# Attention times a gated network on one core: two projections moved behind the last layer, the warming matmuls split, weight blocks moved on GpSimd

## The chip, the cores and the metric

The kernel runs on one NeuronCore of one Trainium2 chip. A NeuronCore has a matrix engine (TensorE, PE in the profile; PEld is its weight load), a vector engine (VectorE, DVE), a scalar engine (ScalarE, ACT), a fourth compute engine (GpSimd, POOL) and a queue that here issues the transfers (SyncE, SP). Each takes its own instructions in order, and they wait for one another by semaphores. SBUF is the working memory, PSUM the memory that TensorE writes.

The metric is device time in microseconds (us), the median over runs. The profile is of one execution, and its span is shorter than that execution's device time by what lies around it.

## The reference

For each of 8 sequences of 512 tokens with 256 features:

```
xn = layernorm(x)
q, k, v = split(xn @ in_proj_w.T)          # 16 heads of 16; q and k are rotated by position
s  = softmax(mask(q k^T / 4)) v            # key at or before the query, fewer than 250 back
s  = s @ out_proj_w.T
h  = relu(s0 * [xn, -xn] @ K0) * 2         # K0, K1, K2 hold +1 or -1
h  = relu(s1 * h @ K1) * 2
g  = silu(s2 * h @ K2)
out = x + s * g
```

Everything is float32.

## The kernel before

**Tiles.** A sequence is worked on transposed: features on the 128 partitions, its 512 tokens along the row. The token tiles of 128 that come in and go out are numbered t = 0 to 3. The layers of the gated network take each weight block twice, against the high half of the activations (float16, names ending in h) and against the low rest (names ending in l), and both products are summed in PSUM. So there are two copies of each sign matrix: w1h and w1l, w2h and w2l.

**Order.** The function run() orders the program. Every piece of work is a triple: planned time in us, its cost on TensorE, and a function that issues instructions. The pieces are sorted by planned time; a piece may return follow-ups with a delay, which wait in a heap until the plan's clock has passed them. The order that comes out is the order on each engine's queue; the planned times are the author's numbers and are not measured. A sequence takes SEQ = 42 plan units; L1, L2 and L3 are the plan's costs of a block of the first, second and third layer.

**PSUM.** The pool ps_m has three buffers (tag "mm"), which almost all products outside attention share: xnT (the transposes), ka, kb, qa, qb (the projections of k and q, two halves each), v_ps, h_ps, z_ps and att_ps. A product can begin only when the buffer that it is given has been emptied. ps_o has one buffer for the attention values.

**The start.** make_identity builds ident on GpSimd. warm (L206) runs 16 matmuls of ident by itself. VectorE takes the mean and variance (stats) and normalises each token tile (norm, L250, name xn), TensorE transposes it (turn_x, xnT_ps), and ScalarE and VectorE take the copies xT, xh and xl out of PSUM. VectorE builds w0h from bytes (make_w0). project() computes ka, kb, qa, qb; VectorE multiplies each by the two rows of the rotation table (L319, names m_ka, m_kb, m_qa, m_qb), and GpSimd's rotate (L339) combines m_ka with m_kb, and m_qa with m_qb. m_kb and m_qb share one buffer, so m_qb can be written only when the rotation of k has read m_kb. ScalarE rounds the rotated k and q (kh, qh, L356), VectorE takes the rests (L363), and they go through DRAM to be laid out for the heads.

make_w1 (L174) turns the bytes of the second layer's weights, kb1, into blocks of w1h or w1l of 128x1024: on ScalarE or on GpSimd (L180). make_w2 (L182) does the same for the third layer on GpSimd (w2h, w2l). Their places are the list at L846. GpSimd also masks the attention's probabilities (L640, L647).

**The end.** For all sequences but the last, the third layer z_ps of a sequence runs inside the next sequence. In the last one (b = 7) the second layer is done in two halves of 256 tokens, each followed by the third layer of its two token tiles. last() (L429) computes z_ps. For t = 0 and 1, VectorE scales it into gate, and gate_ready() forms the sigmoid: exponential on ScalarE, plus one on GpSimd, reciprocal on VectorE (L505), product on GpSimd (L506). project_o() (L778) computes att_ps, the output projection, and loads x again as xr; the product with gate is taken on VectorE (L795), the sum with xr on GpSimd (L800), and SyncE stores the tile (L801). For t = 2 and 3 ("final") the projection is done before z_ps and copied out as att (L791), and behind z_ps follow on VectorE: the product of z_ps, scale and att (L451), the reciprocal (L461), a product (L462) and a sum (L463), and the store (L464). late() (L518) gives the projections' planned times: for the last sequence

```
        if b + 1 == B:
            return SEQ * b + 40.0 + 0.9 * t
```

xr has two buffers: the load for tile 2 waits until tile 0 has been summed.

Of the kernel before, what the change touches and what calls it, by code (L numbers as in the profile page):

```python
# [11 lines left out]
F32 = mybir.dt.float32  # L12
# [4 lines left out]
ALU = mybir.AluOpType  # L17
# [17 lines left out]
def tile_attention_times_gated_ffn(  # L35
# [37 lines left out]
    nc = tc.nc  # L73
    P = 128
    B, T, E = x.shape
    H = HEADS
    D = E // H
    NT = T // P
# [14 lines left out]
    work = ctx.enter_context(tc.tile_pool(name="work", bufs=2))  # L93
# [109 lines left out]

    quick = set()

    def warm():  # L206

        pw = ps_m.tile([P, P], F32, tag="mm", name="warm")
        for n in range(16):
            nc.tensor.matmul(pw, ident, ident, start=(n == 0), stop=(n == 15))  # L210

    def run(pieces):
        clock, count_, due = 0.0, itertools.count(), []
# [215 lines left out]
    def last(b, t, how):  # L429
        st = states[b]  # L430
        pz = ps_m.tile([P, E], F32, tag="mm", name=f"z_ps_{b}_{t}")
        if how == "at once":
            for c in range(NF1):
                nc.tensor.matmul(
                    pz, st["h2p"][:, c, ts(t, P)], w2["l"][:, c].bitcast(F32),
                    start=(c == 0), stop=(c == NF1 - 1),
                )
        else:
            for p in "hl":
                for c in range(NF1):  # L440
                    nc.tensor.matmul(  # L441
                        pz, st["h2" + p][:, c, ts(t, P)], w2[p][:, c],
                        start=(c == 0 and p == "h"), stop=(c == NF1 - 1 and p == "l"),
                    )
        gate = st["gate", t] = outs.tile([P, E], F32, tag=f"gate{t}", name=f"gate_{b}_{t}")
        if how == "final":
            den = denominator(b, t)

            def ends():
                nc.scalar.activation(den, pz, AF.Exp, scale=scales[:, 1:2])  # L450
                nc.vector.scalar_tensor_tensor(  # L451
                    gate, pz, scales[:, 0:1], st["att", t], ALU.mult, ALU.mult
                )
                return [(0.5, add)]

            def add():
                nc.scalar.activation(den, den, AF.Identity, bias=1.0)
                return [(0.4, final)]

            def final():  # L460
                nc.vector.reciprocal(den, den)  # L461
                nc.vector.tensor_tensor(gate, gate, den, ALU.mult)  # L462
                nc.vector.tensor_tensor(gate, gate, st["xr", t], ALU.add)  # L463
                nc.sync.dma_start(out[b, ts(t, P), :], gate)  # L464

            return [(0.0, ends)]

        def scale():
            nc.vector.tensor_scalar(gate, pz, scales[:, 0:1], None, ALU.mult)
            if how != "later":  # L470
                return [(0.5, lambda: gate_ready(b, t))]

        return [(0.0, scale)]

# [45 lines left out]

    def late(b, t):

        if b + 1 == B:
            return SEQ * b + 40.0 + 0.9 * t
        return SEQ * (b + 1) + (32.0 + 3.2 * t if b + 2 < B else 18.0 + 2.5 * t)
# [252 lines left out]
    def project_o(b, t, final=False):  # L778
        st = states[b]
        pp = ps_m.tile([P, E], F32, tag="mm", name=f"att_ps_{b}_{t}")  # L780
        for c in range(EC):
            nc.tensor.matmul(  # L782
                pp, st["V", c][:, ts(t, P)], wo_sb[:, c, :],
                start=(c == 0), stop=(c == EC - 1),
            )
        xr = work.tile([P, E], F32, tag="xr", name=f"xr_{b}_{t}")
        nc.sync.dma_start(xr, x[b, ts(t, P), :])
        st["xr", t] = xr
        if final:
            att = st["att", t] = work.tile([P, E], F32, tag="xn", name=f"att_{b}_{t}")  # L790
            return [(0.0, lambda: nc.scalar.copy(att, pp))]  # L791

        def product():
            y = st["gate", t]
            nc.vector.tensor_tensor(y, pp, y, ALU.mult)  # L795
            return [(0.5, store)]

        def store():
            y = st.pop(("gate", t))
            nc.gpsimd.tensor_tensor(y, y, xr, ALU.add)  # L800
            nc.sync.dma_start(out[b, ts(t, P), :], y)  # L801

        return [(0.0, product)]
# [31 lines left out]
    def swap():  # L835
# [2 lines left out]
        outs = ctx.enter_context(tc.tile_pool(name="outs", bufs=1))  # L838

    everything = [  # L840
        (-38.5, 0, signs), (-40.5, 0, warm),
        (18.2, 0, make_w2), (22.5, 0, swap), (SEQ * (B - 1) + 45.0, 0, add_up),
    ]
    for c in range(EC):
        everything.append((-30 + 0.1 * c, 0, lambda c=c: make_w0(c)))
    for w, f, at, engine in (  # L846
        ("l", 0, -20, nc.gpsimd), ("l", 1, -19, nc.gpsimd), ("l", 2, -18, nc.gpsimd),
        ("h", 0, -17, nc.scalar), ("h", 1, -16, nc.scalar), ("h", 2, 5, nc.gpsimd),
        ("l", 3, 9.0, nc.gpsimd), ("l", 4, 9.1, nc.gpsimd), ("l", 5, 9.2, nc.gpsimd),
        ("l", 6, 9.3, nc.gpsimd), ("l", 7, 9.4, nc.gpsimd), ("h", 3, 15.2, nc.scalar),  # L850
        ("h", 4, 17.0, nc.scalar), ("h", 5, 18.7, nc.scalar), ("h", 6, 20.4, nc.scalar),
        ("h", 7, 22.2, nc.scalar),
    ):
        everything.append((at, 0, lambda f=f, w=w, e=engine: make_w1(f, w, e)))
# [139 lines left out]
```

## Time and profile before

| | |
|---|---|
| Device time, three runs | 629.59, 631.65, 631.93 us; median 631.65 |
| Profiled execution, device time | 632.4 us |
| Its span | 630.6 us |
| TensorE busy | 609.6 us, 97% of the span |
| VectorE busy | 393.0 us, 62% |
| GpSimd busy | 316.1 us, 50% |
| ScalarE busy | 300.0 us, 48% |
| Largest group, L415 h_ps by float32 halves of w1 | 576 matmuls of 392 ns mean |
| GpSimd waits for ScalarE's p before a mask (L640), longest | 9.1 us |

The busy time of an engine is how long some instruction of it ran, and the share is that of the whole span. A mean share doesn't say which engine a given stage waits for; that is read from the waits (who waited, for whom, how long), from the timeline (start in us from the span's start, length, engine, source line, operation, output<-inputs, and in brackets the idle time before it and what ended it), and from the chain (the work that ended last, followed back). The table by stretch gives, for stretches of time, each engine's busy us and number of instructions, the clock granted to TensorE as a share of full speed, and the share and speed of the transfers. A float32 matmul appears as two passes.

### The profile page before, as it was taken

The page shows a single profiled execution, that of the slowest core. Times are in us where ns is not written, and L with a number is a line of the kernel's source. Part 1 is how long each engine was busy: PE and PEld are TensorE (multiplying, and loading weights), DVE is VectorE, ACT ScalarE, POOL GpSimd, SP SyncE. Part 2 cuts the span into 40 slices and gives each one's busy share as a digit, 9 for nine tenths or more (in the row PEclk, how much of TensorE's full clock was granted, in tenths as well). Part 3 has the DMA queues.
Part 4 walks back from the last instruction along what each step waited for, and adds up shares of the span by engine and source line. Part 5 has one row for each costly group of instructions (what it writes and reads, how often), then busy time and mean ns, then how long its engine had stood idle before and what let it go on. Part 6 is the DMA issues. An engine that isn't in the chain of part 4 may idle for free.

```text
span 630.6 us, 12029 instructions
## 1 busy us (share of the span) xinstructions
PE 609.6 (97%) x4834; PEld 398.8 (63%) x4834; DVE 393.0 (62%) x668; ACT 300.0 (48%) x442; POOL 316.1 (50%) x406
## 2 busy tenths in 40 slices
PE   7899999999999999999999999999999999999993
PEld 5454566656665567755676566765676556777883
DVE  6582545757656674766758576485675668457664
ACT  3566564525455445535355454453444544564421
POOL 1945452356623566327644367234662356638630
PEclk9899999999999999999999999999999999999998
DMA  8261821125321163113521153402532116230101
GB/s 269 81 234 51 300 86 50 36 83 210 101 76 50 68 223 112 51 51 144 166 93 51 55 221 96 132 25 94 207 107 73 51 68 226 76 109 18 53 26 40
DMA packets 38193, 67.20 MB, mean 107 GB/s; under 512 B 5104, under 2 KB 19184, under 8 KB 38128
## 3 DMA queue, kind: packets, MB, share of 16 engines
q1 hardware_dynamic: 36384, 64.24, 30.2%
q10 hardware_dynamic: 1744, 2.10, 1.0%
q8 instruction: 40, 0.66, 0.4%
q14 instruction: 25, 0.20, 0.1%
HBM read 36.96 MB, written 29.36 MB: 105 GB/s over the span
## 4 chain that ended last, share of the span: by engine, by line
PE 84%; DVE 6%; DMA 4%; POOL 3%; ACT 2%; issue 1%; SPq 0%; POOLq 0%; ACTq 0%
PE h_ps L415 40%; PE po L679 11%; PE z_ps L441 9%; PE sc L605 7%; PE v_ps L292 4%; PE att_ps L782 4%; PE qa_ps L307 2%; PE kb_ps L307 2%; PE qb_ps L307 2%; DMA kb<-in_k_dram 2%; DMA xr<-in_x_dram 2%; PE ka_ps L307 2%; PE xnT_ps L268 1%; DVE den L505 1%; ACT p L624 1%
## 5 line engine op out<-in xcount | busy, mean ns | idle before, releaser
L624 ACT ACTIVATE p<-sc 128x1024 f32<-128x1024 f32 (+2 forms) x144 | 138.5, 1013 | 75.0 <-PE sc L605 41.0
L640 POOL TENSOR_SCALAR_AFFINE_SELECT p<-p 128x512 f32<-128x512 f32 x128 | 93.8, 739 | 106.5 <-ACT p L624 106.5
L415 PE MATMUL h_ps<-h1l,w1l_sb 128*128 128x512 f32 (+1 forms) x576 | 144.2, 392 | 0.0
L415 PE MATMUL h_ps<-h1h,w1h_sb 128*128 128x512 f16 (+1 forms) x576 | 123.0, 356 | 0.9 <-ACT v_pad L299 0.5
L415 PEld LDWEIGHTS h_ps<-h1l,w1l_sb 128*128 128x128 f32 x576 | 99.5, 188 | 25.7 <-issue 6.8
L426 ACT ACTIVATE h2h<-h_ps 128x512 f16<-128x512 f32 (+1 forms) x72 | 39.6, 550 | 136.5 <-PE h_ps L415 136.4
L415 PEld LDWEIGHTS <-w1h_sb 128*128 128x128 f16 x576 | 51.6, 98 | 55.8 <-issue 14.0
L647 POOL TENSOR_SCALAR_AFFINE_SELECT p<-p 128x512 f32<-128x512 f32 (+1 forms) x96 | 50.4, 525 | 58.0 <-ACT p L624 56.7
L679 PE MATMUL po<-p,v_pad 128*32 128x378 f32 (+4 forms) x1216 | 77.0, 372 | 1.6 <-DVE S L703 1.1
L424 DVE SCALAR_TENSOR_TENSOR h2l<-h_ps,h2h 128x512 fp32r<-128x512 f32 (+1 forms) x72 | 44.4, 617 | 52.0 <-ACT h2h L426 52.0
L505 DVE RECIPROCAL den<-den 128x256 f32<-128x256 f32 x30 | 52.5, 1749 | 26.0 <-POOL den L501 26.0
L424 DVE SCALAR_TENSOR_TENSOR h1l<-h_ps,h1h 128x512 fp32r<-128x512 f32 x64 | 42.5, 675 | 36.1 <-ACT h1h L426 36.1
L605 PEld LDWEIGHTS sc<-q,k 32*128 32x128 f32 x1216 | 44.1, 184 | 26.1 <-issue 15.0
L754 DVE RECIPROCAL S<-S 128x128 f32<-128x128 f32 x64 | 58.9, 934 | 0.0
L426 ACT ACTIVATE h1h<-h_ps 128x512 f16<-128x512 f32 x64 | 38.2, 597 | 43.0 <-PE h_ps L415 42.8
L605 PE MATMUL sc<-q,k 32*128 32x378 f32 (+4 forms) x1216 | 57.3, 306 | 0.0
L415 PE MATMUL h_ps<-xl,w0l_sb 128*128 128x512 f32 x128 | 53.6, 500 | 0.0
L679 PEld LDWEIGHTS po<-p,v_pad 128*32 128x32 f32 x1216 | 31.5, 109 | 30.8 <-issue 16.6
L800 POOL TENSOR_TENSOR gate<-gate,xr 128x256 f32<-128x256 f32 x30 | 23.1, 770 | 46.7 <-DMA xr<-in_x_dram 32.6
L415 PE MATMUL h_ps<-xh,w0h_sb 128*128 128x512 f16 x128 | 39.5, 391 | 0.1
L441 PE MATMUL z_ps<-w2l_sb,h2l 128*128 128x256 f32 x256 | 38.1, 291 | 0.0
L339 POOL TENSOR_TENSOR m_ka<-m_ka,m_kb 128x512 f32<-128x512 f32 x16 | 20.1, 1276 | 30.3 <-DVE m_kb L319 30.3
(95 smaller groups left out, 806.6 us busy)
## 6 DMA issues: line engine op xcount, KB each, us to landing
q<-dq SPq DMA_DIRECT2D x64, 256.0 KB, 3.5
dq<-qh SPq DMA_DIRECT2D x16, 512.0 KB, 3.4
dq<-m_qa SPq DMA_DIRECT2D x16, 512.0 KB, 4.6
k<-dk SPq DMA_DIRECT2D x32, 256.0 KB, 2.8
dk<-kh SPq DMA_DIRECT2D x8, 512.0 KB, 2.7
dk<-m_ka SPq DMA_DIRECT2D x8, 512.0 KB, 2.7
xr<-in_x_dram SPq DMA_DIRECT2D x32, 128.0 KB, 2.3
out_dram<-gate SPq DMA_DIRECT2D x32, 128.0 KB, 1.7
```

Source lines behind the costliest of these rows:

```text
L307: nc.tensor.matmul(ps, wqkv_sb[:, c, ds(col, P)], st["xT"][:, c, :], start=(c == 0), stop=(c == EC - 1),)
L415: nc.tensor.matmul(ph, w[p][:, c, ts(f, P)], st[src + p][:, c, cols], start=(k == 0), stop=(k == n - 1),)
L424: nc.vector.scalar_tensor_tensor(lo, ph, 0.0, hi, ALU.max, ALU.subtract)
L426: high = lambda: nc.scalar.activation(hi, ph, AF.Relu)
L441: nc.tensor.matmul(pz, st["h2" + p][:, c, ts(t, P)], w2[p][:, c], start=(c == 0 and p == "h"), stop=(c == NF1 - 1 and p == "l"),)
L505: nc.vector.reciprocal(den, den)
L605: nc.tensor.matmul(sc[r // 2][:, r % 2, ds(off, n)], st["k0", g][row, ts(j, P)], st[f"q{turn}", g][row, ds(j * P + first, n)], start=(turn ...
L624: nc.scalar.activation(p[:, 2 * half : 2 * half + 2, :n], sc[half][:, :, :n], AF.Exp, scale=D ** -0.5,)
L640: nc.gpsimd.affine_select(out=block, in_=block, compare_op=ALU.is_ge, fill=0.0, base=0, pattern=[[0, 4], [1, P]], channel_multiplier=-1,)
L647: nc.gpsimd.affine_select(out=block, in_=block, compare_op=ALU.is_ge, fill=0.0, base=-1, pattern=[[0, 4], [-1, beyond]], channel_multiplier=1,
L679: nc.tensor.matmul(po[32 * r : 32 * r + 32, ds(j * P + first, n)], v_columns(j, g, r), p_[:, r, ds(off, n)], start=(j == 0), stop=(done an ...
L754: nc.vector.reciprocal(part, part)
```

## The change

It has three parts.

1. Weight blocks of w1 on GpSimd: of the three float32 blocks l 0, l 1, l 2 that stood first, l 2 goes behind the rotation of k. The blocks l 3, l 4, l 5 keep their place behind the rotation of q, and l 6 and l 7 go behind make_w2. make_w2 itself and the second sequence's statistics come ahead of these two.
2. warm is called three times: 12 matmuls where there were 16, 3 behind the second pair of transposes, 5 behind the fourth. They write the attention's PSUM buffer in place of one of ps_m.
3. In the last sequence, the projections of the tiles 2 and 3 go behind the third layer. Tile 2 now uses product() and store() as the tiles 0 and 1 do, with its gate multiplied by den on GpSimd beforehand. Tile 3 has its projection copied by ScalarE, multiplied into gate by GpSimd, and the product with den and the sum with xr are VectorE's. The sigmoid of tile 1 is formed later: its reciprocal stands behind three h2l on VectorE, not before them.

On SyncE, the load of xr for tile 2 now stands behind the store of tile 1, and the store of tile 3 ahead of that of tile 2.

```
-    def warm():
-
-        pw = ps_m.tile([P, P], F32, tag="mm", name="warm")
-        for n in range(16):
-            nc.tensor.matmul(pw, ident, ident, start=(n == 0), stop=(n == 15))
+    def warm(count_):
+
+        pw = ps_o.tile([P, P], F32, tag="po", name="warm")
+        for n in range(count_):
+            nc.tensor.matmul(pw, ident, ident, start=(n == 0), stop=(n == count_ - 1))
...
                 nc.scalar.activation(den, pz, AF.Exp, scale=scales[:, 1:2])
-                nc.vector.scalar_tensor_tensor(
-                    gate, pz, scales[:, 0:1], st["att", t], ALU.mult, ALU.mult
-                )
-                return [(0.5, add)]
+                nc.vector.tensor_scalar(gate, pz, scales[:, 0:1], None, ALU.mult)
+                return [(0.3, add)]
 
             def add():
                 nc.scalar.activation(den, den, AF.Identity, bias=1.0)
-                return [(0.4, final)]
-
-            def final():
+                return [(0.3, invert_)]
+
+            def invert_():
                 nc.vector.reciprocal(den, den)
-                nc.vector.tensor_tensor(gate, gate, den, ALU.mult)
-                nc.vector.tensor_tensor(gate, gate, st["xr", t], ALU.add)
-                nc.sync.dma_start(out[b, ts(t, P), :], gate)
+                if t + 1 < NT:
+                    nc.gpsimd.tensor_tensor(gate, gate, den, ALU.mult)
+                st["den"] = den
...
-                return [(0.5, lambda: gate_ready(b, t))]
+                return [(0.5 if t == 0 else 4.5, lambda: gate_ready(b, t))]
...
+        if b + 1 == B and t >= NT // 2:
+            return last_at(b, NT - 1) + L3 + 0.9 * (t - NT // 2)
         if b + 1 == B:
...
-        if final:
-            att = st["att", t] = work.tile([P, E], F32, tag="xn", name=f"att_{b}_{t}")
-            return [(0.0, lambda: nc.scalar.copy(att, pp))]
+        if final and t + 1 == NT:
+            att = work.tile([P, E], F32, tag="xn", name=f"att_{b}_{t}")
+
+            def out_of_psum():
+                y, den = st["gate", t], st["den"]
+                nc.scalar.copy(att, pp)
+                nc.gpsimd.tensor_tensor(y, y, att, ALU.mult)
+                nc.vector.tensor_tensor(y, y, den, ALU.mult)
+                nc.vector.tensor_tensor(y, y, xr, ALU.add)
+                nc.sync.dma_start(out[b, ts(t, P), :], y)
+
+            return [(0.0, out_of_psum)]
...
-            return [(0.5, store)]
+            return [(1.0 if final else 0.5, store)]
...
-        (-38.5, 0, signs), (-40.5, 0, warm),
-        (18.2, 0, make_w2), (22.5, 0, swap), (SEQ * (B - 1) + 45.0, 0, add_up),
+        (-38.5, 0, signs), (-40.5, 0, lambda: warm(12)), (-34.5, 0, lambda: warm(3)),
+        (-32.5, 0, lambda: warm(5)),
+        (19.2, 0, make_w2), (22.5, 0, swap), (SEQ * (B - 1) + 45.0, 0, add_up),
...
-        ("l", 0, -20, nc.gpsimd), ("l", 1, -19, nc.gpsimd), ("l", 2, -18, nc.gpsimd),
-        ("h", 0, -17, nc.scalar), ("h", 1, -16, nc.scalar), ("h", 2, 5, nc.gpsimd),
-        ("l", 3, 9.0, nc.gpsimd), ("l", 4, 9.1, nc.gpsimd), ("l", 5, 9.2, nc.gpsimd),
-        ("l", 6, 9.3, nc.gpsimd), ("l", 7, 9.4, nc.gpsimd), ("h", 3, 15.2, nc.scalar),
+        ("l", 0, -20, nc.gpsimd), ("l", 1, -19, nc.gpsimd), ("l", 2, 5.1, nc.gpsimd),
+        ("h", 0, -17, nc.scalar), ("h", 1, -16, nc.scalar), ("h", 2, 5.2, nc.gpsimd),
+        ("l", 3, 11.8, nc.gpsimd), ("l", 4, 11.9, nc.gpsimd), ("l", 5, 12.0, nc.gpsimd),
+        ("l", 6, 19.3, nc.gpsimd), ("l", 7, 19.4, nc.gpsimd), ("h", 3, 15.2, nc.scalar),
```

## The prediction

> **What bounds the kernel now.** I read the page's first part, then its chain, the waits of TensorE, the timeline of the first 50 us and of the last 30, and the table by stretch around the first pauses.
>
> ```profile
> PE 609.6 (97%) x4834; PEld 398.8 (63%) x4834; DVE 393.0 (62%) x668; ACT 300.0 (48%) x442; POOL 316.1 (50%) x406
> ```
>
> TensorE is busy for 609.6 of 630.6 us, so an edit pays only where TensorE waits, or has nothing left to do. Of its waits (what waited, for what; us in total, times, longest) these two matter here; the first is the longest inside the program:
>
> ```profile
> PE v_ps L292 <- DVE m_qb L319: 2.3, 1, 2.3
> PE h_ps L415 <- DVE h2l L424: 0.5, 1, 0.5
> ```
>
> The timeline (start, length, engine) shows whose wait the first is:
>
> ```profile
> 15.94 3.56 POOL L180 TENSOR_SCALAR w1l_sb<-kb,sgn,sgnn 128x1024 fp32r<-128x1024 uint8 x3 [8.62 <-DMA kb<-in_k_dram]
> 19.46 2.51 POOL L339 TENSOR_TENSOR m_ka<-m_ka,m_kb 128x512 f32<-128x512 f32 x2
> 22.00 1.29 DVE L319 TENSOR_TENSOR m_qb<-qb_ps,rope_sb 128x512 f32<-128x512 f32 x2 [3.20 <-POOL m_ka L339]
> 23.35 1.16 PE L292 MATMUL v_ps<-wqkv_sb,xT 128*128 128x256 f32 x4 [2.33 <-DVE m_qb L319]
> ```
>
> GpSimd starts three weight blocks when kb1 lands, 1.20 us each, and only then rotates k (m_ka). VectorE's m_qb overwrites the buffer that this rotation reads, so it starts at 22.00; v_ps needs the PSUM buffer that m_qb empties, so TensorE stands from 21.01 to 23.35. The other input of the rotation, m_kb, was ready at 17.09. GpSimd's queue is the bound here, not TensorE. The table by stretch (time, busy us of PE, PEld, DVE, ACT, POOL, granted clock) shows a second price of this pause:
>
> ```profile
> 17.49:20.90 3.41, 3.41 (x12) 1.47 (x11) 1.29 (x2) 1.25 (x2) 3.41 (x4) 1.00 0.00 1
> 20.90:24.32 3.42, 1.09 (x6) 0.78 (x6) 2.31 (x4) 0.60 (x1) 3.42 (x3) 1.00 0.00 0
> 24.32:27.73 3.41, 3.41 (x9) 1.97 (x8) 0.86 (x2) 1.85 (x3) 3.41 (x4) 0.50 0.00 0
> 27.73:31.14 3.41, 3.41 (x17) 2.46 (x16) 2.64 (x4) 2.13 (x6) 3.41 (x3) 1.00 0.75 297
> ```
>
> After the stretch with only 1.09 us of matmuls the clock is halved for 3.41 us; after stretches with 2.59 us of 3.41 (31.14 to 34.55) it isn't. The tail, from the chain in order of time:
>
> ```profile
> 601.78 1.61 DVE den L505
> 603.72 3.80 PE h_ps L415 x32
> 610.20 1.73 PE att_ps L782 x8
> 613.74 0.86 PE att_ps L782 x4
> 616.55 1.94 PE z_ps L441 x16
> 619.56 1.73 DVE den L461
> 622.59 1.67 DVE den L461
> 624.75 0.42 DVE gate L463
> ```
>
> The last z_ps ends at 620.31, but VectorE works on until 625.17: per tile a product, a reciprocal of 1.75, a product, a sum, two tiles in series. The last store is issued at 625.20 and the span ends 5.4 us later. Two projections of 0.86 us each (at 610.9 and 613.6) stand ahead of z_ps, and at 603.3 a reciprocal holds up h2l and TensorE behind it.
>
> **What the Trainium skill says.** "TensorE: Matmul & The Clock Gate", Part 1 on the HAM clock gate: activity is judged in free-running windows of 3413 ns, and an idle window halves the clock. The trace agrees: the passes of warm start 0.213 us apart up to 7.18 and 0.112 after, and the half-clock stretch is 3.41 long. It doesn't show how little activity is too little; I take something between 1.09 and 2.59 us. "SBUF — State Buffer", section "Who interferes with whom": GpSimd and a two-port (or, against a GpSimd reader, two-input) VectorE operation exclude one another for whole instructions. The trace agrees:
>
> ```profile
> 36.42 2.69 DVE L250 TENSOR_SCALAR xn<-x,mv,rstd 128x256 f32<-128x256 f32 x2
> 34.46 2.61 POOL L184 TENSOR_SCALAR w2h_sb<-kb 128x2048 f16<-128x2048 uint8 x1
> 37.04 1.93 POOL L184 TENSOR_SCALAR w2l_sb<-kb 128x2048 fp32r<-128x2048 uint8 x1
> ```
>
> Two L250 of 0.40 took 0.79 and 1.98 us and ended just behind w2h and w2l; w2h took 2.61 behind a two-input L363, its like 1.93.
>
> **Part 1: fewer early blocks.** One of the three blocks leaves the front: the rotation starts at 18.30 instead of 19.46, ends at 20.81, m_qb ends at 22.13, v_ps starts at 22.18. That is 1.17 us. The block isn't gone: it goes behind the k rotation, ahead of block h 2, and fills 20.8 to 22.0, so the q rotation starts at 23.12 as before. m_qa isn't needed before ACT's qh at 31.12, so this costs nothing; without that cover it would cost 1.17.
>
> Follow the chain on. v_ps 22.18, h_ps 2 ends at 24.21, ACT's kh 24.7 to 25.8. VectorE's L363 (two inputs) then meets a GpSimd block that began at 25.6 and waits to 26.8, ending at 27.9 (before: 29.04, after the same wait in the next block). h1l 3 follows to 28.5. Next VectorE waited 0.69 us for h1h 4 (from 29.65 to 30.34); with a full clock that h_ps ends near 26.9, so this idle time goes too. From h1l 4 on VectorE runs without a gap to v_ps at 34.23 (before). So the lead there is 1.17 + 0.7 = 1.9 us. If the clock is halved all the same, 1.2; if L363 gets in ahead of the block at 25.6 (it is 0.2 late), one block more, 3.1. I take 1.9: the new pause is 1.17 us, so the busy time of any window is at least 2.2 us, near the 2.59 that kept the clock.
>
> Blocks l 6 and l 7 go behind w2h and w2l: 2.4 us of GpSimd more in front of the first mask, which cover: GpSimd is idle for 9.1 us ahead of 48.09. But now they hold the port while sequence 1 is normalised. VectorE got in between w2h and w2l, so the third xn waits at most for the rest of one block, and xnT has about 0.9 us in hand: nothing. Below nothing is excluded, as nothing leaves. The upper bound is the slow rival.
>
> **Part 2: warm in three pieces.** 16 matmuls become 12 + 3 + 5. Twelve are 24 passes and end at 7.7; xn arrives at 8.62, when the old 16 had just ended: no gain, no loss. Three more (6 x 0.112 = 0.7 us) move the third xnT from 9.63 to about 10.0; ACT reads it from 10.42, now 10.5. Five more (1.1 us) push ka from 11.50 to 12.0, ending at 13.9. VectorE is in w0h and xl until 14.04 and then takes ka, and kb waited for xl until 13.78 anyway: nothing. Cover gone, it is 0.5; with a half clock, m_kb could come 1.2 later and still meet the rotation at 18.30.
>
> **Part 3: the tail.** Removed from in front of z_ps: 2 x 0.863 = 1.73 us. The reciprocal of den 1 moves behind three h2l: h2l 0 comes at 602.05 instead of 603.67, and the fourth h_ps starts at 603.11 (its three predecessors start 1.83 apart) instead of 603.72: 0.61. So z_ps of tile 3 ends 2.34 earlier, at 617.97; the moved reciprocal delays h2l 3 to 606.1, needed at 607.6.
>
> From there, with the durations of the same rows: Exp ends 616.70 and 618.54, plus one 617.15 and 619.00, VectorE: gate 2 to 617.22, reciprocal to 618.93, gate 3 to 619.30, reciprocal to 621.0. Meanwhile TensorE does the two projections, to 618.84 and 619.71, ACT copies the last to 620.12, GpSimd multiplies gate 2 by den (from 618.97) and gate 3 by att (to 620.9), 0.73 each. Then on VectorE: gate 2 by att_ps to 621.33, gate 3 by den to 621.69, plus xr to 622.1; on GpSimd gate 2 plus xr. The last two meet on the port: one waits 0.6. Stores are issued by 622.55 to 623.15, against 625.20: gain 2.05 to 2.65. Two stores in 0.4 us instead of 3 apart may land up to 0.3 later. I take 2.2 (1.7 to 2.7).
>
> SP: xr 2 now stands behind the store of tile 1. That store waits for xr 1, which took 3.7 us to land; xr 2 and 3 are then issued by 615 and are needed at 621.4. Loads of this row took 2.0 to 5.8 us: covered.
>
> **Sum.** 1.9 + 2.2 = 4.1 us of the profiled execution's 632.4 (span 630.6 and 1.8 around it), giving 628.3. That execution lies 0.75 above the median of the runs shown, 631.65; against the median, 627.6. Between start and tail TensorE has next to no waits, so a lead is handed through.
>
> **The rivals.** *Start gain eaten* (0.25): L363 or the half clock leaves 1.2 or less, the port in the tail costs its 0.6: 2.0 to 3.1 us, 628.6 to 629.6. For it: VectorE's waits come in steps of one GpSimd block. Against: those 0.7 us idle at 29.65.
> *More than forecast* (0.17): L363 slips in ahead, 3.1 + 2.6 = 5.7 us, 625.9. Against it: 0.2 us late.
> *Slower* (0.08): the port. If GpSimd, with l 6 and l 7 queued, isn't interrupted between blocks, the second xn of sequence 1 waits 2 x 1.2 us more, xnT and everything queued on TensorE behind it too, the pause closes the clock for a window (1.7 us): 4.1 and more lost. It turns the sum from the point where both blocks pass ahead of one xn, with any loss beside it: about 632. Against: the interleaving at 37.04.
> *Not what it says*: the warm pieces do nothing visible, as the clock is full from 7.25; that is in all cases.
>
> **How the numbers follow.** The forecast, 3.2 to 4.9 us, has 0.50. 0.5% is 3.2 us, about what a measurement of this kernel can tell from no change. Faster: 0.48 of the forecast and 0.17. Same: 0.24 of the eaten case, 0.02 of the forecast and 0.03 of the slow one. Slower: what is left of the eaten case (0.01) and of the slow one (0.05), 0.06. The range, 625.4 to 630.4, holds the forecast and both gaining rivals with the 2 us by which the runs shown differ; it leaves the slow case out.
>
> **What would show it.** m_ka from 18.3 and v_ps from 22.2; no half clock at 24 to 28; L363 of k ending near 27.9; v_ps 3 at 32.3; no wait at h_ps near 603; z_ps ending 4.2 us earlier on the trace's scale; last store 4.1 us earlier. The prediction is wrong if the clock is halved elsewhere near the start, if L250 of sequence 1 lasts beyond 2 us, or if the last VectorE or GpSimd sum waits for xr.

## The result, and the profile after

The changed kernel takes 628.59 us (median of 20 runs, 627.96 to 630.13); the kernel before, run beside it on the same chip, takes 631.39 (median of 20, 629.59 to 632.57). The ratio is 0.9964 with a 95% interval of 0.9956 to 0.9971, a gain of 1.8 to 2.8 us, 2.3 in the middle. The time lies inside the range given, 1.0 above the forecast of 627.6, and the ratio is inside the half per cent that I had called no change, which had 0.29. The gain of 3.2 to 4.9 us that I had held likeliest, with 0.50, did not come.

The runs below take the parts one by one. Parts 1 and 3 gain 1.8 us each, near what was forecast (1.9 and 2.2). Part 2, which I had at nothing, **costs** 1.5. Without it the other two gain 3.9 us by the medians, 3.3 by the ratio.

The page of the changed kernel, first part: busy time, share of the span, instructions.

```profile
PE 608.6 (97%) x4842; PEld 398.4 (64%) x4842; DVE 394.1 (63%) x667; ACT 299.7 (48%) x441; POOL 316.2 (50%) x409
```

TensorE has 8 matmuls' records more than before (each of the 4 added matmuls runs as two passes), and is about as busy as it was, 608.6 us for 609.6: the gain comes out of its waits and out of the end. The waits of TensorE in the changed kernel (what waited, for what; us in total, times, longest):

```profile
PE v_ps L292 <- DVE h1l L424: 1.6, 2, 0.8
PE v_ps L292 <- DVE m_qb L319: 1.3, 1, 1.3
...
PE z_ps L441 <- DVE h2l L424: 0.4, 1, 0.4
```

The pause ahead of v_ps fell from 2.3 to 1.3 us. The wait of h_ps for h2l, 0.5 us near 603, is gone, as forecast. The last line is new: TensorE waits for h2l of the *last sequence* at z_ps, 0.4 us, in a stretch that I had taken to be free of waits. The timeline of the start (start, length, engine):

```profile
15.23 2.38 POOL L180 TENSOR_SCALAR w1l_sb<-kb,sgn,sgnn 128x1024 fp32r<-128x1024 uint8 x2 [7.92 <-DMA kb<-in_k_dram]
17.57 2.51 POOL L339 TENSOR_TENSOR m_ka<-m_ka,m_kb 128x512 f32<-128x512 f32 x2
20.12 1.29 DVE L319 TENSOR_TENSOR m_qb<-qb_ps,rope_sb 128x512 f32<-128x512 f32 x2 [2.18 <-POOL m_ka L339]
21.46 1.13 PE L292 MATMUL v_ps<-wqkv_sb,xT 128*128 128x256 f32 x4 [1.32 <-DVE m_qb L319]
```

Two blocks stand ahead of the rotation instead of three. Measured from the landing of kb1 (the start of the first block, which differs by up to 0.8 us from one execution to the next), v_ps starts at 6.23 us; in the kernel before it was 23.35 - 15.94 = 7.41. That is 1.18 us, and 1.17 were forecast. The table by stretch over the same pause (time, busy us of PE, PEld, DVE, ACT, POOL, granted clock, DMA):

```profile
17.20:20.60 3.40, 2.94 (x11) 1.26 (x9) 1.22 (x3) 1.26 (x3) 3.40 (x4) 1.00 0.00 0
20.60:24.00 3.40, 2.54 (x11) 1.75 (x12) 2.00 (x4) 1.02 (x3) 3.40 (x4) 1.00 0.00 0
24.00:27.40 3.40, 3.09 (x14) 1.83 (x12) 3.00 (x3) 2.69 (x6) 3.40 (x3) 1.00 0.41 161
```

The granted clock stays at 1.00. The first score matmul comes 26.06 us after kb1, where it was 27.98 in the execution shown before: 1.92, the forecast's 1.9. The blocks that moved behind w2h and w2l, from the timeline again:

```profile
31.82 2.61 POOL L184 TENSOR_SCALAR w2h_sb<-kb 128x2048 f16<-128x2048 uint8 x1
33.79 2.69 DVE L250 TENSOR_SCALAR xn<-x,mv,rstd 128x256 f32<-128x256 f32 x2
34.40 1.93 POOL L184 TENSOR_SCALAR w2l_sb<-kb 128x2048 fp32r<-128x2048 uint8 x1
36.32 2.52 POOL L180 TENSOR_SCALAR w1l_sb<-kb,sgn,sgnn 128x1024 fp32r<-128x1024 uint8 x2
```

The two normalisations L250 took 2.69 us together, exactly as before, and the two blocks came behind w2l, at 36.32, when the second normalisation was nearly over (36.48). The slow rival, which lived on this place, did not happen. The chain in order of time (start, length, what), first near the new wait, then in the tail:

```profile
587.35 0.73 POOL gate L809
588.09 1.24 POOL V L763
589.41 1.50 POOL R L767
591.64 0.35 DVE h2l L424
592.03 0.39 PE z_ps L441
...
604.65 0.86 PE att_ps L782 x4
607.33 0.86 PE att_ps L782 x4
...
611.97 1.94 PE z_ps L441 x16
613.99 0.48 ACT den L450
616.92 1.74 DVE den L459
618.86 0.42 DVE gate L796
619.30 0.83 DVE gate L797
```

Two att_ps projections stand ahead of the last z_ps instead of four. From the first h_ps of the second half of the last sequence's second layer (at 595.35 here) to the start of that layer's last matmul it is 16.21 us for 18.52 before: 2.31, where 2.34 was forecast. But the first five lines say that TensorE entered this stretch with less lead than it had won. The lead over the kernel before, h_ps by h_ps, was 2.64 at 33 us, 3.07 at 163, 2.93 at 445 and 2.27 at 595; then 2.88 at 601 and 4.58 at the last. So 0.8 us had gone between 163 and 595, all but 0.14 of it behind 588, and the chain names the way: a sum on GpSimd (L809) late, its products V and R late behind it, VectorE's R and h2l late behind those, z_ps last.

### The profile page after: what moved, and what is told of

The parts are those of the page before. It is cut to its first block, busy times and chain, and to the rows that moved or that the text cites. A ratio compares the mean times of both kernels' runs of the same rounds, so it can differ in the third digit from the quotient of the medians.

```text
span 626.6 us, 12051 instructions
## 1 busy us (share of the span) xinstructions
PE 608.6 (97%) x4842; PEld 398.4 (64%) x4842; DVE 394.1 (63%) x667; ACT 299.7 (48%) x441; POOL 316.2 (50%) x409
## 4 chain that ended last, share of the span: by engine, by line
PE 85%; DVE 5%; POOL 3%; DMA 3%; ACT 2%; issue 1%; SPq 0%; POOLq 0%; ACTq 0%; DVEq 0%
PE h_ps L415 41%; PE po L679 11%; PE z_ps L441 9%; PE sc L605 8%; PE v_ps L292 4%; PE att_ps L782 4%; PE qa_ps L307 2%; PE kb_ps L307 2%; PE qb_ps L307 2%; DMA kb<-in_k_dram 2%; PE ka_ps L307 2%; PE xnT_ps L268 1%; DVE den L503 1%; DVE h2l L424 1%; DVE xn L250 1%
## 5 line engine op out<-in xcount | busy, mean ns | idle before, releaser
L640 POOL TENSOR_SCALAR_AFFINE_SELECT p<-p 128x512 f32<-128x512 f32 x128 | 90.3, 711 | 104.0 <-ACT p L624 104.0
L809 POOL TENSOR_TENSOR gate<-gate,xr 128x256 f32<-128x256 f32 x31 | 25.1, 810 | 46.8 <-DMA xr<-in_x_dram 41.2
```

The lines of the kernel that those rows point to most:

```text
L640: nc.gpsimd.affine_select(out=block, in_=block, compare_op=ALU.is_ge, fill=0.0, base=0, pattern=[[0, 4], [1, P]], channel_multiplier=-1,)
```

## The experiments

Every kernel was run as the two above, beside the kernel before on the same chip. "Gain" below is 631 us times the distance of the ratio from 1, with the interval in brackets; the medians stand beside it. The two differ somewhat, as the kernel before scatters by 3 to 4 us. The rows follow the experiments below.

| kernel | median | before beside it | ratio, 95% interval | gain, us |
|---|---|---|---|---|
| part 1 alone | 629.57 | 630.97 | 0.9971 (0.9961 to 0.9982) | 1.8 (1.1 to 2.5) |
| part 3 alone | 629.56 | 630.97 | 0.9972 (0.9959 to 0.9985) | 1.8 (0.9 to 2.6) |
| part 2 alone | 632.76 | 630.97 | 1.0024 (1.0015 to 1.0032) | -1.5 (-2.0 to -0.9) |
| before, 8 + 3 + 5 matmuls | 630.84 | 631.30 | 0.9994 (0.9986 to 1.0001) | 0.4 (-0.1 to 0.9) |
| before, 20 matmuls in one piece | 631.72 | 631.30 | 1.0015 (1.0005 to 1.0025) | -0.9 (-1.6 to -0.3) |
| changed, 8 + 3 + 5 matmuls | 627.85 | 631.30 | 0.9949 (0.9933 to 0.9965) | 3.2 (2.2 to 4.2) |
| before, 6 of the 16 in the pause | 630.74 | 631.30 | 0.9995 (0.9985 to 1.0006) | 0.3 (-0.4 to 0.9) |
| parts 1 and 3 | 626.99 | 630.93 | 0.9947 (0.9933 to 0.9962) | 3.3 (2.4 to 4.2) |
| parts 1 and 3, two blocks more behind | 627.53 | 630.93 | 0.9952 (0.9938 to 0.9967) | 3.0 (2.1 to 3.9) |
| parts 1 and 3, store on ScalarE | 627.62 | 630.93 | 0.9957 (0.9943 to 0.9972) | 2.7 (1.8 to 3.6) |
| parts 1 and 3, both | 627.70 | 630.93 | 0.9958 (0.9944 to 0.9972) | 2.7 (1.8 to 3.5) |

### Each part alone

**Part 1 alone**, the list of blocks:

```diff
-        (18.2, 0, make_w2), ...
+        (19.2, 0, make_w2), ...
-        ("l", 0, -20, nc.gpsimd), ("l", 1, -19, nc.gpsimd), ("l", 2, -18, nc.gpsimd),
-        ("h", 0, -17, nc.scalar), ("h", 1, -16, nc.scalar), ("h", 2, 5, nc.gpsimd),
-        ("l", 3, 9.0, nc.gpsimd), ...
+        ("l", 0, -20, nc.gpsimd), ("l", 1, -19, nc.gpsimd), ("l", 2, 5.1, nc.gpsimd),
+        ("h", 0, -17, nc.scalar), ("h", 1, -16, nc.scalar), ("h", 2, 5.2, nc.gpsimd),
+        ("l", 3, 11.8, nc.gpsimd), ...
```

> Part 1 alone: weight block l 2 behind the rotation of k, l 6 and l 7 behind w2. Theory A (the start is worth what the two profiles show): v_ps begins about 6.4 us after kb1 lands instead of 7.6, the clock isn't halved, 1.9 us less than before in the median. Rival B (the profiled execution of before was one of the slower ones, with its half clock and late kb1; the usual one loses less): 0.8 to 1.3 us less. Rival C (the whole missing part lies in the tail): 1.9 here, and tail_only below 1.

Measured: 1.8 us gained, v_ps 6.22 and the first score matmul 26.03 us after kb1, clock at full. The lead of the start is handed through: 1.93 us at 34 us, 1.79 at 596.

**Part 3 alone**, all hunks of the last layer, of its sigmoids and of the last projections, on the kernel before; two of them:

```diff
+        if b + 1 == B and t >= NT // 2:
+            return last_at(b, NT - 1) + L3 + 0.9 * (t - NT // 2)
...
-            return [(0.4, final)]
+            return [(0.3, invert_)]
```

> Part 3 alone: the two projections behind the third layer, the sigmoid of tile 1 later. Theory A: as forecast 2.2 us less (1.7 to 2.7), with the last store issued 2.0 to 2.6 us earlier on the trace's scale. Rival C: the two stores at the end land later than one did and return most of it, below 1.0 us less. Rival B: 1.6 to 2.2 us less.

Measured: 1.8 us gained. From the first h_ps of the second half to the last one it is 16.20 us for 18.52: all of the 2.3. Some of it is given back behind z_ps: the two stores are issued 0.45 us apart instead of 3, the second took 0.96 us to issue (0.34 before), and the span ends 5.46 us after that issue, 5.16 to 5.39 in the seven profiles of kernels without part 3.

**Part 2 alone**, the three pieces of warm on the kernel before:

```diff
-    def warm():
-        pw = ps_m.tile([P, P], F32, tag="mm", name="warm")
-        for n in range(16):
+    def warm(count_):
+        pw = ps_o.tile([P, P], F32, tag="po", name="warm")
+        for n in range(count_):
...
-        (-38.5, 0, signs), (-40.5, 0, warm),
+        (-38.5, 0, signs), (-40.5, 0, lambda: warm(12)), (-34.5, 0, lambda: warm(3)),
+        (-32.5, 0, lambda: warm(5)),
```

> Part 2 alone: 12 + 3 + 5 warming matmuls in place of 16. All theories: no difference, within 0.3 us. If it costs 0.5 us or more, the forecast's cover (VectorE in w0h until ka is taken) is gone in usual executions, and part of the missing gain is here.

Measured: 1.5 us *slower*. Nothing shows near the pieces: v_ps starts 7.39 us after kb1, for 7.41 in the kernel before. Its waits of TensorE have the line that the changed kernel has, and larger:

```profile
PE z_ps L441 <- DVE h2l L424: 0.7, 1, 0.7
```

So the wait came with part 2, a change at 3 to 12 us, and appeared at 596. **The kernel before, profiled once more**, as a control:

> The kernel before once more, for a second profile. Theory A: again a stretch of 3.4 us at half clock behind the pause at v_ps. Rival B: no half clock this time, since the windows run freely against the program; kb1 lands at another moment than 15.75 and v_ps and the end move with it.

Measured: 630.68 us (one run), span 628.95, against 630.59 in the profile that the prediction was read from. It has no wait at z_ps, and no half clock. v_ps starts 7.41 us after kb1, as in the first profile, but the first score matmul 27.21 after it instead of 27.98. So the half clock behind the pause isn't in every execution, and where it is, it costs 0.8 us up to the first score matmul.

### What part 2 does: its number or its places

Part 2 splits the matmuls, which also moves them to the attention's PSUM buffer, and it makes 20 of 16. **The split alone**, with part 2's warm(count_) and that buffer, on the kernel before:

```diff
-        (-38.5, 0, signs), (-40.5, 0, warm),
+        (-38.5, 0, signs), (-40.5, 0, lambda: warm(8)), (-34.5, 0, lambda: warm(3)),
+        (-32.5, 0, lambda: warm(5)),
```

> The kernel before with warm in three pieces of 8 + 3 + 5, so that TensorE's program has as many instructions as before. Theory F (the four matmuls that 12 + 3 + 5 adds shift every later fetch of TensorE's instructions, and one of these then meets a load of xr; the pieces' places cost nothing): no difference from before, within 0.5 us, and no wait of z_ps near 596. Rival G (the pieces among the transposes cost): 1 us or more above before, as with 12 + 3 + 5.

**The number alone**, in one piece in front and in the old buffer:

```diff
-        for n in range(16):
-            nc.tensor.matmul(pw, ident, ident, start=(n == 0), stop=(n == 15))
+        for n in range(20):
+            nc.tensor.matmul(pw, ident, ident, start=(n == 0), stop=(n == 19))
```

> The kernel before with 20 warming matmuls in one piece at the front, in ps_m as before. Theory F: as with 12 + 3 + 5 the fetches come about 1 us earlier, 1.0 to 1.8 us above before, the load of xr for tile 2 of sequence 6 lands late and z_ps waits near 596. Rival G: no more than 0.5 us above before.

**The changed kernel with 16 in its three pieces:**

```diff
-        (-38.5, 0, signs), (-40.5, 0, lambda: warm(12)), (-34.5, 0, lambda: warm(3)),
+        (-38.5, 0, signs), (-40.5, 0, lambda: warm(8)), (-34.5, 0, lambda: warm(3)),
```

> The changed kernel with 8 + 3 + 5. Theory F: 0.8 to 1.6 us below the changed kernel's 628.6, 3.4 to 4 below before. Rival G: within 0.5 us of the changed kernel.

Measured: 16 in pieces costs nothing (0.4 gained, -0.1 to 0.9), 20 in one piece costs 0.9 (0.3 to 1.6), and the changed kernel gains 0.9 by taking four away (628.59 to 627.85 by the medians, ratios 0.9964 and 0.9949). The intervals of the first two don't touch, so it is the number. The third points the same way, though its interval and that of the changed kernel overlap. The half clock (below) isn't the reason: among the runs with a listed clock of 0.994 or more, the kernel before takes 630.51 us on the mean, 16 in pieces 630.63, 20 in one piece 631.72.

Where it costs shows when the profiles are laid side by side. From the first score matmul to the first h_ps of the second half of the last sequence's second layer, a stretch in which no part of the change moves anything, the eleven profiles with 16 have 552.76 to 553.85 us, mean 553.36; the three with 20 have 554.06, 554.23 and 555.08, mean 554.46. That is 1.1 us, and it is not at the front. Most of it lies at the end: from the last sequence's first h_ps of that layer, near 564 us, to the same mark it is 31.48 to 31.71 us with 16, without a wait at z_ps, and 32.19 (the changed kernel), 32.50 (part 2 alone) and 32.09 (20 in one piece) with 20, with waits of 0.4, 0.7 and 0.3. Ahead of that the two groups overlap.

Part 2 changes no instruction in that stretch. What differs is which transfers meet. SyncE issues the loads of the residual rows all through the kernel; but instructions are fetched by DMA too, and the profile lists a queue for them. In the page of the changed kernel (queue, kind: packets, MB, share):

```profile
q8 instruction: 40, 0.66, 0.4%
```

Forty fetches of 16 KB, one every 15.3 us on the mean. They are TensorE's program: from one to the next, the end left out, TensorE runs 256 recorded instructions on the mean (255.8 to 256.9 in the fourteen profiles, four intervals in five between 224 and 287), and no other engine's count is as even. The answers for the tile xr between 575 and 595 us, where four of these loads lie (how long GpSimd sat idle until one landed, and how often; then the time from issue to landing): first the changed kernel, then the kernel before with part 2, both with 20 matmuls.

```profile
  DMA xr<-in_x_dram: 2.9, 1
...
DMA to landing us min/median/max: 2.0/2.1/3.2
```

```profile
  DMA xr<-in_x_dram: 3.2, 1
...
DMA to landing us min/median/max: 2.1/2.2/3.6
```

And with 16: the kernel before with 8 + 3 + 5. Parts 1 and 3 (below) have the same two lines.

```profile
  DMA xr<-in_x_dram: 1.8, 1
...
DMA to landing us min/median/max: 2.1/2.1/2.2
```

The last number of each second line is the slowest of four loads of 128 KB. In these two kernels with 16 matmuls all four land within 2.2 us; with 20 one of them takes 3.2 or 3.6, and GpSimd's sum waits 1.1 to 1.4 us longer for it. By the trace's records of the transfers the late one is the third tile of sequence 6 (issued at 580.23 in the changed kernel), and a fetch begins 0.77 us behind its issue. The same load in all fourteen profiles: in the three with 20 the fetch begins 0.77, 0.80 and 0.95 us behind the issue and the sum waits 2.8 to 3.2 us; in the eleven with 16 it begins 1.66 to 2.18 behind and the sum waits 1.8 to 2.4. There the load has nearly landed when the fetch comes. The fetch took 0.95 to 1.33 us. GpSimd works in order, so behind the late sum stand L763 and L767, and behind those VectorE's R, h2l and TensorE, as the chain above has it.

Why four matmuls shift the fetches: they sit at the head of TensorE's program, so every later 16 KB ends that much earlier in the work. The four are 16 records, 8 matmuls and 8 weight loads. Counted in records from the first score matmul, the mean place of the fetches agrees within 4 records among the eleven profiles with 16, and lies 14 records earlier in the three with 20 (single fetches scatter more). At 15.3 us for 256 records, 14 to 16 are an estimated 0.8 to 1.0 us; against the issue of the load the fetch came 1.0 us earlier than with 16 (means of 0.84 and 1.81 us).

That a fetch delays a load isn't a matter of this one load. Of the 448 residual loads in the fourteen profiles, 266 had none of the program's transfers beside them in their first 2.5 us, stores and other residual loads left aside. The 51 with a fetch that began 0 to 1.25 us behind their issue took 2.57 to 4.10 us to land, median 3.40; the 133 with no fetch from 2 us before to 4 us behind it took 2.02 to 2.53, median 2.17. With 20 matmuls three loads are late in all three profiles (near 236, 382 and 582 us: 3.1 to 3.6 us) that land in 2.1 to 2.8 in all eleven with 16. But a late load need not cost: the one near 532 is late in all fourteen, 3.2 to 3.7 us, and neither in the changed kernel nor in parts 1 and 3 does a wait of TensorE follow it before 560.

So it is shown that the number costs, that it moves the fetches, and that a load beside a fetch lands late; from the late load to z_ps the chain above leads. No run moved a fetch without moving instructions, and how a fetch delays a load is open. Part 2 alone lost 1.0 us at z_ps, and another 0.6 between 385 and 404, where GpSimd waited 2.44 us for a load that took 3.4.

### The half clock

**Six of the 16 matmuls in the pause**, on the kernel before with part 2's warm(count_), to keep the clock up:

```diff
-        (-38.5, 0, signs), (-40.5, 0, warm),
+        (-38.5, 0, signs), (-40.5, 0, lambda: warm(10)), (9.19, 0, lambda: warm(6)),
```

> The kernel before with 10 of its 16 warming matmuls at the front and 6 in TensorE's pause ahead of v_ps (1.35 us of its 2.3), all else alike. If the half clock behind the pause is in most executions of before and costs 0.8 us (the difference of two profiles of before, counted from the landing of kb1): 0.5 to 0.8 us less than before, and no half clock in the profile. If it is rare: no difference, within 0.3 us. If it costs all of its 1.7 us: 1.2 to 1.7 us less.

Measured: no gain (0.3, -0.4 to 0.9), and the experiment is confounded. With only ten in front, the clock fell to half from 9.11 to 15.93 instead. After it the clock was full through the pause, v_ps started 8.37 us after kb1 (six matmuls more in front of it), and the first score matmul 27.21 after kb1, exactly as in the execution of the kernel before without a half clock. In this execution the six matmuls in the pause spent what the clock would have cost.

How often is the clock halved? Each timed run lists its mean granted clock. Of 51 runs of the kernel before, beside the second group of kernels, 23 have 0.993 or less and 28 have 0.994 or more; averaged clock by clock, the first take 631.66 to 632.37 us, the second 630.05 to 630.96. Of the 36 beside the first three kernels 14 have 0.993 or less, of the 11 beside the last four 3. The split isn't sharp: the profile of part 3 alone has the half clock behind the pause and lists 0.994. All 20 runs of the changed kernel and all 11 of part 1 alone have 0.994 or more, and none of the seven profiles with part 1 has the half clock there; of the seven without it, three have. So part 1 does take the half clock away, but by this split it was there in only 40 of 98 runs: 1.2 us always, and 0.7 more where the clock would have been halved.

### Parts 1 and 3, and two steps beyond

If part 2 costs and the others gain, the two without it must beat the changed kernel. **Parts 1 and 3** with the warm of before, one piece of 16:

```diff
-        (-38.5, 0, signs), (-40.5, 0, lambda: warm(12)), (-34.5, 0, lambda: warm(3)),
-        (-32.5, 0, lambda: warm(5)),
+        (-38.5, 0, signs), (-40.5, 0, warm),
```

> Parts 1 and 3 of the change without part 2: the warm-up matmuls stay one piece of 16 in front, as in the kernel before. If part 2 costs by its four added matmuls, which shift the instruction fetches onto the loads of the residual rows, this comes 3.2 to 3.6 us below the kernel before and about 1 below the changed one, with no wait of the last layer's projection near 592 us. If the lead is lost in the end of the last tile instead, whatever the front looks like, it comes within 0.3 of the changed kernel, 2.3 to 2.8 below before.

Measured: 626.99 us, six runs from 626.55 to 627.47, all below the fastest of the 20 runs of the changed kernel (627.96). By the medians 3.9 us are gained, by the ratio 2.4 to 4.2. No wait at z_ps; v_ps 6.22 us after kb1, the first score matmul 26.03. Over the changed kernel with 8 + 3 + 5 it gains 0.9 by the medians but 0.1 by the ratios, so a difference isn't shown. The profiles have one: with 8 in front the clock was full only from 14.31 us (7.20 in the changed kernel with 12, 7.25 in the kernel before with 16), the projections ended late, and the first score matmul came 26.61 us after kb1. In the kernel before with 8 + 3 + 5 the clock was full from 11.20, and there it cost nothing (27.20 us after kb1).

**Two blocks more behind the rotation of k:**

```diff
-        ("l", 0, -20, nc.gpsimd), ("l", 1, -19, nc.gpsimd), ("l", 2, 5.1, nc.gpsimd),
+        ("l", 0, 5.02, nc.gpsimd), ("l", 1, 5.04, nc.gpsimd), ("l", 2, 5.1, nc.gpsimd),
```

> Parts 1 and 3, with the layer-weight blocks l 0 and l 1 also put behind the rotation of k. If GpSimd's blocks ahead of the rotation set the end of the pause, v_ps starts when k's and q's projections are ready: 5.0 to 5.2 us after the first block of the k weight, for 6.2 with part 1 alone and 7.4 before, and the time is 1.0 to 1.2 below parts 1 and 3. If the moved blocks only hold up what comes behind them (the rotation of q, or VectorE through the shared port), v_ps moves but the first score matmul does not, and the time is within 0.3 of parts 1 and 3.

Measured: 627.53, no gain (0.5 above parts 1 and 3 by the medians, the intervals overlap). The pause is gone, and the time came back at once. (The first weight block no longer marks the landing of kb1 here, so times are counted from q's second projection.) The waits of TensorE in this kernel from 17 to 35 us, then in parts 1 and 3:

```profile
PE v_ps L292 <- DVE h1l L424: 2.5, 2, 1.7
```

```profile
PE v_ps L292 <- DVE h1l L424: 1.6, 2, 0.8
PE v_ps L292 <- DVE m_qb L319: 0.7, 1, 0.7
```

What holds h1l up, from the timeline of the kernel with the blocks moved, then of parts 1 and 3:

```profile
24.19 2.52 POOL L339 TENSOR_TENSOR m_qa<-m_qa,m_qb 128x512 f32<-128x512 f32 x2
24.80 3.01 DVE L363 TENSOR_TENSOR m_ka<-m_ka,kh 128x1024 fp32r<-128x1024 f32 x1 [0.24 <-ACT kh L356]
```

```profile
22.57 2.51 POOL L339 TENSOR_TENSOR m_qa<-m_qa,m_qb 128x512 f32<-128x512 f32 x2
25.25 2.10 DVE L363 TENSOR_TENSOR m_ka<-m_ka,kh 128x1024 fp32r<-128x1024 f32 x1 [0.24 <-ACT kh L356]
```

GpSimd's rotation of q now starts at 24.19, 0.61 us ahead of VectorE's two-input L363 at 24.80. That one ends at 27.81, 1.1 us behind the rotation, having taken 3.01 us where it took 2.10 in parts 1 and 3; h1l and v_ps wait behind it. From the start of q's second projection to the first score matmul it is 24.14 us, and 24.22 with the pause. The Trainium skill ("SBUF — State Buffer", "Who interferes with whom") says that the engine which issues first keeps the shared pair for its whole instruction and the other one blocks: L363 shows it, at 3.01 us for the 1.22 that the same operation takes undisturbed for q at 32.08. The second of the two expectations was right: v_ps came 3.53 us behind q's second projection instead of 4.42, and the score matmul stayed where it was.

**The last store on ScalarE's queue:**

```diff
-            nc.sync.dma_start(out[b, ts(t, P), :], y)
+            (nc.scalar if final else nc.sync).dma_start(out[b, ts(t, P), :], y)
```

> Parts 1 and 3, with the store of the last tile issued from ScalarE's queue in place of SyncE's; the other store stays. If the two stores stand in each other's way at SyncE (the second took 0.95 to 1.14 us to issue, 0.34 before), the time is 0.3 to 0.7 below parts 1 and 3, and the issue takes 0.4. If the landing sets the end, or the issue is long wherever it is, the time is within 0.2 of parts 1 and 3.

This is the store of tile 2, the later of the two in SyncE's queue. Measured: 627.62, no gain (0.6 above by the medians). The issue did become short. The timeline of this kernel, and that of the changed kernel with both stores on SyncE:

```profile
619.55 0.37 ACTq L810 DMA_DIRECT2D out_dram<-gate  x1
619.83 0.35 SPq L798 DMA_DIRECT2D out_dram<-gate  x1
```

```profile
620.16 0.35 SPq L798 DMA_DIRECT2D out_dram<-gate  x1
620.61 1.14 SPq L810 DMA_DIRECT2D out_dram<-gate  x1
```

SyncE's end came 4.2 us after the last issue, 4.7 in parts 1 and 3. But in the trace's closing records ScalarE reaches its end 3.4 us later than in parts 1 and 3 (623.39 for 619.97), and after GpSimd's last step at 624.6 nothing moves until ScalarE's at 625.55; in parts 1 and 3 the same step follows at once, 0.08 later. From the end of z_ps to the end of the span it is 10.50 us, and 10.41 there. In the kernel with both steps it is the same: 0.90 us of waiting for ScalarE, and 10.55 us. Neither expectation named this. Why ScalarE's end is slow when it has issued a store last is open.

**Both:**

> Parts 1 and 3 with both further edits, the two blocks behind the rotation of k and the last store on ScalarE's queue. If both gains are real and start and tail are apart, the sum of the two: 1.3 to 1.9 us below parts 1 and 3, about 626. If the earlier start is lost to late residual loads between, it is no better than the better of the two.

Measured: 627.70, as either alone; neither gain was real, so there was nothing to add. Parts 1 and 3 is the best of all kernels run.

## Why the prediction was right or wrong

**Part 1, right.** 1.17 us at v_ps was forecast; it is 1.18 between profiles. The 0.7 more, from the full clock and VectorE's idle time, is there (1.92 up to the first score matmul), but only against an execution with the half clock; against one without it is 1.15 to 1.18. I took one execution's half clock for the kernel's. The Trainium skill ("TensorE: Matmul & The Clock Gate", Part 1) says that the windows run free and that the phase differs from run to run; I cited the section and did not draw that consequence. With the half clock in about 0.4 of the runs, 1.2 and 0.4 x 0.7 are 1.5; measured are 1.8 (1.1 to 2.5), which can't tell 1.5 from my 1.9. The cover for l 6 and l 7, and for the order of h 2, held.

**Part 2, wrong; this is the step that failed.** "Nothing" was right at the place where I had priced it: the three pieces are over at 7.8, 9.2 and 11.2 us, ka starts at 11.06 and the projections are done before the rotation of k, as the sum had it. It failed because I priced the added matmuls by their passes (8 x 0.11 us under cover) and the loads by their queues, and took the instruction stream to be free. Four matmuls more in front move the 40 fetches of the program against the 32 residual loads, and in this kernel onto three that they missed with 16: 1.5 us when alone (0.9 to 2.0), 1.1 in the profiles' stretch between start and tail.

**"A lead is handed through", wrong with it.** TensorE has next to no waits between start and tail only while the residual load ahead of V, R and h2l lands in time. Of the 3.07 us of lead at 163 us, 0.8 were gone at 595. In part 1 alone and in parts 1 and 3 the sentence holds.

**Part 3, right in the mechanism, short in one term.** The last layer is 2.31 us shorter for 2.34 forecast, with 0.6 from the reciprocal and 1.71 from two projections. From the last z_ps of tile 3 to the issue of the last store the two kernels agree (4.89 before, 4.88 after, the two sums side by side with 0.83 us each for 0.42 and 0.73). The term that was too small is the landing: the "up to 0.3 later" is 0.57 in the profile of the changed kernel (5.96 us from the last issue to the end of the span, 5.39 before) and 0.1 to 0.3 in four other kernels with part 3. In all five the second store took 0.92 to 1.14 us to issue, and in all five a 16 KB fetch was under way then. The fetch alone isn't the reason: with the other store on ScalarE's queue, SyncE's took 0.35 us at 619.83 with a fetch under way, too. What makes the second of two long is open. The whole part gains 1.8 (0.9 to 2.6) of 2.2.

**The sum.** 1.8 + 1.8 - 1.5 = 2.1, measured 2.3 (1.8 to 2.8); forecast 4.1. The time lies in the range because the range was wide enough for two rivals; none of them named this loss, so that is luck. Parts 1 and 3 alone, measured at 3.3 (2.4 to 4.2) and 3.9 by the medians, come near what I forecast for the whole. The two profiles shown differ by 632.4 - 628.36 = 4.0 us, which looks like the forecast come true. It isn't: 0.7 of it is an earlier kb1, 0.8 a half clock that more than half of the runs, by the clock they list, don't have.

**The rivals.** *Start gain eaten* had the right size, 2.0 to 3.1 us, for the wrong reason: L363 did not slip back and the clock was not halved. *Slower by the port* did not come: GpSimd was interrupted between blocks as at 37.04 before. *More than forecast* did not come either: in the changed kernel L363 stood behind the first of three blocks as forecast. The port bound returned only where two more blocks were moved.

## What to carry to other kernels

Price an instruction that is added on a busy engine for the whole program, not only at its place: here it shifted the program's own fetches against every load behind it. When a small edit at the front changes a wait hundreds of us later, change the number of instructions by itself before looking for a reason in the work. Look at two or three executions of the kernel before, and at the clock listed with each run, before you count a half-clock stretch as something to gain. And when a pause is priced by the work ahead of it, ask which engine is next to be late: the second step of the same kind here gained nothing, as VectorE and GpSimd were already back to back on their shared port.

## What the runs showed that I had not expected

- A program of 4,842 matmuls arrives in 40 fetches of 16 KB, about 15 us apart, 0.9 to 1.6 us each in the changed kernel. A 128 KB load with a fetch up to 1.25 us behind its issue landed after 3.40 us in the median of 51; with none near it, after 2.17.
- Busy time alone doesn't tell when the clock is halved. In windows of 3.41 us counted from the clock's own changes, it was halved behind one with 1.36 us of matmuls (part 2 alone, first two lines) and not behind one with 1.63 (the kernel before once more); but in the kernel with six of the matmuls in the pause it was halved near the front, behind one with 1.87, made of matmuls and transposes 128 columns wide.

```profile
19.53:22.94 3.41, 1.36 (x6) 0.50 (x5) 1.10 (x2) 1.19 (x2) 3.41 (x3) 1.00 0.00 0
22.94:26.35 3.41, 3.17 (x8) 2.15 (x8) 1.38 (x3) 0.37 (x1) 3.41 (x4) 0.50 0.00 0
```

```profile
21.16:24.57 3.41, 1.63 (x7) 1.25 (x8) 2.48 (x4) 0.81 (x2) 3.41 (x4) 1.00 0.00 0
24.57:27.98 3.41, 3.41 (x17) 2.19 (x16) 2.10 (x2) 2.60 (x5) 3.41 (x4) 1.00 0.19 74
```

```profile
5.69:9.11 3.42, 1.87 (x13) 1.33 (x13) 2.49 (x14) 0.63 (x2) 1.05 (x1) 1.00 0.95 340
9.11:12.52 3.41, 2.59 (x6) 1.17 (x6) 3.21 (x5) 3.12 (x8) 0.00 (x0) 0.50 1.10 342
```

- ScalarE, given the last store, issued it in 0.37 us where SyncE took 0.92 to 1.14, but in both kernels with this edit the others then waited for ScalarE's end, 0.95 and 0.90 us.
